# Softplus steps of a selective-scan loop respaced between two engines, D u moved to ScalarE, and a leaner near part

## The chip, the cores and the metric

The kernel runs on one core of a Trainium2 chip. The metric is the device time in microseconds (us) of one execution; the time of a version is the median of its runs. The kernel before takes 2176.8 us, the median of 3 runs from 2174.62 to 2178.04. The profile is of one execution, whose span from the first to the last instruction is 2175.0 us.

Engines are named as in the profile: PE is TensorE, PEld its weight loads, DVE is VectorE, ACT is ScalarE, POOL is GpSimd, and SP is SyncE, which issues the DMAs.

## The reference, cut to what matters

Two layers follow each other on an image x of 64 x 64 pixels with 96 channels. Each normalizes in 32 groups, runs a two-dimensional selective scan (SS2D) and adds the result to x:

```python
x = x + L0(_gn(x))            # softplus, cumulative-sum form, 4 directions, same weights
x = x + L1(_gn(x))            # 4 directions, weights of their own, snake orders

# the core of L1, for direction k, channel d, state n, position t
xz = x @ in_proj_w.T;  xin, z = split(xz)
u  = silu(conv3x3_depthwise(xin) + conv_b)            # 192 channels
dt_r, Bs, Cs = split(x_proj_weight[k] @ u)            # 6 + 16 + 16 rows
delta = softplus(dt_projs_weight[k] @ dt_r + bias[k])
h = h * exp(delta * A) + (delta * u) * B              # A = -exp(A_log), 16 states
y = sum over n of h * C   +   D * u
# then: the four directions are added, layer norm, times silu(z), out_proj
```

In layer 0 the state is written as decay * cumsum(dB_u / (decay + 1e-12)) with decay = exp(cumsum(delta A)), so that positions far along a direction add nothing once the decay has vanished.

## The kernel before, in words

**Layout.** The 192 channels are three tiles T of 128 partitions, each with 64 channels for the upper and the same 64 for the lower half of the image. The 16 states are 8 pairs m.

**Stages.** Each layer has a head (`head`, L885), a scan part and a tail. The head projects, convolves on VectorE (`conv`, L965), applies silu on ScalarE (L981) and starts the output y with D u: `start_y` (L882), called at L986 with GpSimd's multiply, profile line L883. Layer 0 has `near_scans` (L241): only the first NEAR = 192 positions of each direction are scanned, and a flag decides whether `far_scans` (L511) has to run as well; in the profile it does not. Layer 1 has `scans` (L629), the long loop. `scan_weights` (L179) loads the scan weights of a layer: for p in 0, 1 (rows or columns) and d in 0, 1 (forward or backward).

**Near part.** The positions of all four directions are gathered into `nus`, projected (`npj`), and softplus is taken on a tile `npd` of 3 x 384 columns (L339 on). delta, its running sum S and delta u are then written into tiles of twice the size by `both` (L235), four DMAs each, on SyncE: `ndt`, `nS`, `ndu`. VectorE's `nnb` (L441) multiplies by `ndu`.

**Scan loop.** 16 groups k (p, d and a chunk c of the image) x 3 tiles T x 8 pairs m make 384 units; within a group a unit has the slot number 0 to 23. For unit j the stages are:

- `fetch_c`: SyncE loads the row of C, `cb`
- `stage_B`: TensorE spreads the row of B into PSUM (L793, one buffer)
- `stage_a`: ScalarE's exponential m (L802, PSUM, two buffers), VectorE's product b (L806)
- `stage_s`: VectorE's scan h (L815, four buffers), ScalarE's copy of the last column (L820)
- `stage_c`: GpSimd's product hc = h C (L824, five buffers)
- `stage_r`: TensorE adds hc to the output `ys` (L840), five units later

**Prelude.** While a group runs, the operands of the next are prepared: copies of u (`us`, L680), the projection `pj` (L691 copies it to `xd`), the rows B and C, two residuals `rs` (L705, L708), and for each T softplus in five steps: `begin` (TensorE's `pd`, L724, then Abs and Relu on ScalarE, L738 and L739), `logarithm` (ScalarE, four operations, L745 to L748), `lost` (GpSimd, w and ln, L751 and L752), `whole` (GpSimd, sp and su, L755 and L756) and `double` (SyncE, eight DMAs). `pj`, `rs` and `pd` share the two PSUM buffers of m. Each step has a slot; at most one step is taken per slot, in order of the list, and the steps of T = 2 belong to the slots of the next group:

```python
(6, 7, 9, 10, 12, 13, 14, 15, 16, 17, 18, 19, 20, 21, 22),
[copies, project, rows, lambda: residual(0), lambda: residual(1), *delta(0), *delta(1)]
...
return early, list(enumerate(delta(2)))
```

The framework then fixes the order of the instructions in each engine's queue when the program is built; each engine takes its queue in that order.

Of the kernel before, what the change touches and what calls it, by code (L numbers as in the profile page):

```python
# [8 lines left out]
F32 = mybir.dt.float32  # L9
BF16 = mybir.dt.bfloat16  # L10
AF = mybir.ActivationFunctionType
# [32 lines left out]
def two_ss2d_layers(  # L44
# [134 lines left out]
    def scan_weights(l):  # L179

        xw, dwb, am = [], [], []
        for p in range(2):
            lp = 2 * l + p
            w = swp.tile([128, 2, 3, NC], F32, tag=f"xw{p}", name=f"xw{lp}")
            v = swp.tile([128, 2, 3, 128], F32, tag=f"dwb{p}", name=f"dwb{lp}")
            e = swp.tile([128, 2, 3, NS + 1], F32, tag=f"ab{p}", name=f"ab{lp}")
            a = swp.tile([128, 2, 2, 3, NP], F32, tag=f"am{p}", name=f"am{lp}")
            nc.vector.memset(v[96:128], 0.0)  # L190
            for d in range(2):
                r = slice(NB + RK * d, NB + RK * d + RK)
                rr = slice(RK * d, RK * d + RK)
                hi = slice(64 * d, 64 * d + 64)
                c0 = NB + 2 * RK + NS * d
                for half in HALF:
                    for to, of in ((slice(0, NC - NS), slice(0, NC - NS)), (slice(NC - NS, NC), slice(c0, c0 + NS))):
                        nc.sync.dma_start(
                            out=w[half, d, 0:2, to],
                            in_=xpw[lp, :, d, of].rearrange("(b p) c -> p b c", b=2),  # L200
                        )
                        nc.sync.dma_start(out=w[half, d, 2, to], in_=xpw[lp, hi, 2, of])
# [13 lines left out]
                    nc.sync.dma_start(out=e[half, d, 2, :], in_=alb[lp, hi, 2, :])  # L216

            for h, half in enumerate(HALF):
                nc.scalar.activation(a[half, 0], e[half, :, :, h:NS:2], AF.Exp)
            nc.vector.tensor_scalar_mul(a[:, 1], a[:, 0], -0.5)  # L220
            nc.vector.tensor_scalar_mul(a[:, 0], a[:, 0], -1.0)
            xw.append(w)
            dwb.append(v)
            am.append(a)
        return xw, dwb, am
# [6 lines left out]
                out=dst[half], in_=rows[q : q + 1, :].to_broadcast(dst[half].shape)  # L232
            )

    def both(dst, src):  # L235

        for half in HALF:
            for h in range(2):
                nc.sync.dma_start(out=dst[half, ..., h, :], in_=src[HALF[h]])

    def near_scans(weights):  # L241

# [4 lines left out]
        with ExitStack() as sc:  # L247
# [40 lines left out]


            ps = pps.tile([128, 2, 512], F32, tag="m", name="npj")[0:NC, :, 0 : 2 * NEAR]  # L290
            for q in range(2):
                for T in range(3):
                    nc.tensor.matmul(
                        ps[:, q], xw[0:64, 0, T, :], us[0:64, T, q],
                        start=(T == 0), stop=(T == 2),
                    )
# [39 lines left out]
                once.tile([128, 3, 2, 2 * NEAR], F32, name=f"n{nm}") for nm in ("dt", "du", "S")  # L336
            )
            load_exp_ln()
            nc.scalar.activation(w, ps, AF.Abs)  # L339
            nc.vector.tensor_scalar_max(v, ps, 0.0)  # L340
            nc.scalar.activation(w, w, AF.Exp, scale=-1.0)
            nc.scalar.activation(t, w, AF.Identity, bias=one)
            nc.scalar.activation(ln, w, AF.Ln, bias=one)
# [2 lines left out]
            nc.vector.tensor_add(v, v, w)  # L346
            nc.vector.tensor_add(v, v, ln)
            table("exp_and_others")
            both(dt, v)
            nc.vector.tensor_tensor_scan(  # L350
                sums.rearrange("p t w -> p (t w)"), steady.rearrange("p t w -> p (t w)"),
                v.rearrange("p t w -> p (t w)"), 0.0, ALU.mult, ALU.add,
            )
            both(S, sums)
            for h, half in enumerate(HALF):
                nc.gpsimd.tensor_mul(dus[half], v[half], us[half, :, h])
            both(du, dus)

            def four(t, T):
# [99 lines left out]
            def add(j):  # L459
                T, ks = units[j]  # L460
                hc = live.pop(j)[4]
                if ks[0] == 0:
                    live["y"] = pps.tile([128, 2, 512], F32, tag="y", name=f"ny{T}")
                ps = live["y"][:, :, 0 : 2 * NEAR].rearrange("p q (d w) -> p q d w", w=NEAR)
                o = 0
                for i in ks:
                    n, m0, m1 = kinds[i]
                    for m in range(m0, m1):
                        for q in range(2):
                            nc.tensor.matmul(  # L470
                                ps[:, q, :, 0:n], fold2,
                                hc[:, o : o + 2 * n].rearrange("p (d w) -> p d w", w=n),
                                start=(m == 0), stop=(m == NP - 1),
                            )
                            o += 2 * n
                if ks[-1] == len(kinds) - 1:
                    yT = y[T]
                    k = NEAR // HW
                    nears = [
                        (yT[HALF[0], 0:NEAR], ps[HALF[0], 0, 0]),  # L480
                        (yT[HALF[1], L // 2 - NEAR :][:, ::-1], ps[HALF[1], 0, 1]),
                    ]
                    for h, half in enumerate(HALF):
                        nears.append(
                            (columns(yT[half], h, slice(0, k)), of_columns(ps[half, 1, 0], h))
                        )
# [142 lines left out]
    def scans(weights):  # L629

        xw, dwb, am = weights
        with ExitStack() as sc:
# [32 lines left out]
            def prelude(k):  # L665
# [53 lines left out]
                def delta(T):  # L719

                    def begin():
                        ps = spare(f"pd{k}_{T}")[:, 0:HT]
                        for h, half in enumerate(HALF):
# [1 line left out]
                                ps[half], dwb[p][96 : NC + 1, d, T, half],  # L725
                                xd[96 : NC + 1, halves[h]], start=True, stop=True,
                            )
                        me["w"], me["ln"], me["t"] = (
                            pre.tile([128, HT], F32, tag=nm, name=f"{nm}{k}_{T}")
                            for nm in ("w", "ln", "t")  # L730
                        )
                        me["sp"], me["su"] = (
                            pre.tile([128, HT], F32, tag=nm, name=f"{nm}{k}_{T}", bufs=2)
                            for nm in ("sp", "su")
                        )

                        def parts_of_v():
                            nc.scalar.activation(me["w"], ps, AF.Abs)  # L738
                            nc.scalar.activation(me["sp"], ps, AF.Relu)  # L739

                        return parts_of_v


                    def logarithm():
                        nc.scalar.activation(me["w"], me["w"], AF.Exp, scale=-1.0)  # L745
                        nc.scalar.activation(me["ln"], me["w"], AF.Ln, bias=one)
                        nc.scalar.activation(me["t"], me["w"], AF.Identity, bias=one)
                        nc.scalar.activation(me["t"], me["t"], AF.Identity, bias=less1)  # L748

                    def lost():  # L750
                        nc.gpsimd.tensor_sub(me["w"], me["w"], me["t"])  # L751
                        nc.gpsimd.tensor_add(me["ln"], me["ln"], me["w"])  # L752

                    def whole():
                        nc.gpsimd.tensor_add(me["sp"], me["sp"], me["ln"])  # L755
                        nc.gpsimd.tensor_mul(me["su"], me["sp"], me["u"][T])  # L756

                    def double():
                        for nm, of in (("dt", "sp"), ("du", "su")):
                            t = me[nm, T] = pre.tile(  # L760
                                [128, TC], F32, tag=f"{nm}{T}", name=f"{nm}{k}_{T}"
                            )
                            both(t.rearrange("p (h t) -> p h t", h=2), me[of])

                    return [begin, logarithm, lost, whole, double]

                early = list(
                    zip(
                        (6, 7, 9, 10, 12, 13, 14, 15, 16, 17, 18, 19, 20, 21, 22),
                        [  # L770
                            copies, project, rows, lambda: residual(0), lambda: residual(1),
                            *delta(0), *delta(1),
                        ],
                    )
                )
# [109 lines left out]
    def head(l, xT, w):  # L885

        ipw_s, v, ds = w["ipw"], w["v"], w["ds"]
        with ExitStack() as sc:
# [76 lines left out]
            def conv(b, s):  # L965
# [232 lines left out]
```

## Time and profile before

| part of the span, us | length | what VectorE is busy in it | what GpSimd is busy in it |
|---|---|---|---|
| 0 to 103, head of layer 0 | 103 | 85.8 | 37.4 |
| 103 to 198, near part | 95 | 48.1 | 37.2 |
| 198 to 250, tail of layer 0 | 52 | 35.4 | 1.3 |
| 250 to 325, head of layer 1 | 75 | 68.4 | 43.9 |
| 325 to 358, first prelude | 33 | 1.6 | 23.2 |
| 358 to 2124, scan loop | 1766 | 1337.7 | 1121.5 |
| 2124 to 2175, tail of layer 1 | 51 | 28.5 | 2.2 |

Busy time is the time in which an engine executes an instruction. A line of the costliest groups reads: source line, engine, operation, output and inputs, shapes, count; then the total busy time and the mean of one in ns; then the idle time of the engine just before these instructions, and what ended most of it. In the timeline a line has start, duration, engine, source line, operation, and in square brackets the idle time before it with what released it. The mean granted TensorE clock is 0.689 of the full one.

### The profile page before, as it was taken

What the parts mean: (1) busy time and instruction counts of PE and PEld (TensorE: products, weight loads), DVE (VectorE), ACT (ScalarE), POOL (GpSimd) and SP (SyncE); (2) the same over time, 40 slices, a digit from 0 to 9 for tenths busy, and PEclk for the clock granted to TensorE, in tenths of its full rate; (3) what the DMA queues carried; (4) which work ended last, traced back from release to release, by engine and by line L of the source; (5) the groups of instructions that cost most, each with busy time, mean ns of one, the idle gap of its engine ahead of it and who ended that gap; (6) DMA issues with size and microseconds to landing.
All of it is one profiled execution on the core that took longest, in us unless ns stands there. A gap on an engine that the chain in (4) does not pass through costs nothing. (4 is left out here: it accounts for less than half of the span.)

```text
span 2175.0 us, 14719 instructions
## 1 busy us (share of the span) xinstructions
PE 1418.6 (65%) x3694; PEld 369.2 (17%) x3694; DVE 1605.4 (74%) x1108; ACT 881.7 (41%) x1386; POOL 1266.7 (58%) x647
## 2 busy tenths in 40 slices
PE   5337725767676757575757667676767676767678
PEld 3214201111111111111111111111111111111113
DVE  7845793867676868686868777777777777777795
ACT  3343425434343434343443435344434343434333
POOL 0741086575656565656657575757575657574760
PEclk8556866757585858585767776766767676767558
DMA  3243115365555647474838374737473737374663
GB/s 78 77 84 87 39 58 128 106 152 130 146 137 137 155 120 171 116 176 103 188 97 190 101 185 106 185 107 175 113 173 106 180 97 182 103 172 117 154 156 116
DMA packets 130912, 282.88 MB, mean 130 GB/s; under 512 B 45520, under 2 KB 48912, under 8 KB 130720
## 3 DMA queue, kind: packets, MB, share of 16 engines
q1 hardware_dynamic: 128704, 281.06, 53.0%
q10 hardware_dynamic: 2112, 0.79, 0.1%
q8 instruction: 31, 0.51, 0.1%
q14 instruction: 65, 0.53, 0.1%
HBM read 215.75 MB, written 12.13 MB: 105 GB/s over the span
## 5 line engine op out<-in xcount | busy, mean ns | idle before, releaser
L824 POOL TENSOR_TENSOR hc<-h,cb 128x1024 f32<-128x1024 f32 x384 | 895.6, 2353 | 210.2 <-DVE h L815 181.9
L815 DVE TENSOR_TENSOR_SCAN h<-m,carry,b 128x1024 f32<-128x1024 f32 x288 | 673.8, 2343 | 240.4 <-POOL hc L824 219.2
L840 PE MATMUL ys<-hc,fold 128*64 128x512 f32 x1536 | 637.8, 871 | 205.5 <-POOL hc L824 204.7
L806 DVE TENSOR_TENSOR b<-B,du 128x1024 f32<-128x1024 f32 x384 | 469.2, 1222 | 144.8 <-PE B L793 87.7
L802 ACT ACTIVATE m<-dt,am 128x1024 f32<-128x1024 f32 x384 | 428.4, 1116 | 261.7 <-DVE h L815 256.5
L793 PE MATMUL B<-B,selh 96*128 96x512 bf16 x768 | 318.2, 508 | 311.2 <-DVE b L806 310.6
L751 POOL TENSOR_TENSOR w<-w,t 128x512 f32<-128x512 f32 x48 | 60.8, 1267 | 435.3 <-ACT t L748 435.3
L815 DVE TENSOR_TENSOR_SCAN h<-m,b 128x1024 f32<-128x1024 f32 x96 | 218.9, 2284 | 74.2 <-POOL hc L824 66.6
L820 ACT COPY carry<-h 128x1 f32<-128x1 f32 x288 | 54.6, 189 | 503.6 <-DVE h L815 503.1
L840 PEld LDWEIGHTS ys<-hc,fold 128*64 128x64 f32 x1536 | 109.4, 176 | 501.4 <-POOL hc L824 316.0
L793 PEld LDWEIGHTS <-selh 96*128 96x128 bf16 x768 | 70.3, 105 | 730.7 <-issue 727.1
L883 POOL TENSOR_SCALAR y<-u,ds 128x1024 f32<-128x1024 f32 x12 | 98.8, 8246 | 86.7 <-ACT u L981 86.7
L979 DVE SCALAR_TENSOR_TENSOR acc<-pad,v,acc 128x1052 f32<-128x1052 f32 x96 | 121.8, 1334 | 0.3
L835 PE MATMUL ys<-y,ident 128*128 128x256 f32 (+1 forms) x144 | 87.6, 717 | 50.1 <-POOL y L883 37.8
L705 PE MATMUL rs<-xd,ident 96*96 96x512 f32 x128 | 87.7, 775 | 26.7 <-DVE h L815 25.5
L724 PE MATMUL pd<-xd,dwb 29*64 29x512 f32 x192 | 69.9, 815 | 18.2 <-ACT B L715 12.3
L715 ACT CAST B<-rs 32x1024 bf16<-32x1024 f32 x48 | 48.1, 1003 | 70.4 <-PE rs L708 69.7
L752 POOL TENSOR_TENSOR ln<-ln,w 128x512 f32<-128x512 f32 x48 | 60.7, 1264 | 3.7
L755 POOL TENSOR_TENSOR sp<-sp,ln 128x512 f32<-128x512 f32 x48 | 60.7, 1266 | 1.3
L680 ACT COPY us<-u 128x256 f32<-128x256 f32 x48 | 16.7, 403 | 96.5 <-POOL su L756 96.5
L738 ACT ACTIVATE w<-pd 128x512 f32<-128x512 f32 x48 | 28.6, 595 | 65.6 <-PE pd L724 62.7
L845 ACT COPY y<-ys 128x256 f32<-128x256 f32 (+1 forms) x72 | 29.5, 444 | 59.7 <-PE ys L840 59.4
(161 smaller groups left out, 1079.8 us busy)
## 6 DMA issues: line engine op xcount, KB each, us to landing
cb<-C SPq DMA_DIRECT2D x768, 256.0 KB
dt<-sp SPq DMA_DIRECT2D x192, 128.0 KB
du<-su SPq DMA_DIRECT2D x192, 128.0 KB
szd<-sz SPq DMA_DIRECT2D x24, 256.0 KB
szt<-szd SPq DMA_DIRECT2D x24, 256.0 KB
xT<-xs SPq DMA_DIRECT2D x8, 384.0 KB
xs<-xT SPq DMA_DIRECT2D x1, 1536.0 KB
xs<-xT SPq DMA_DIRECT2D x8, 192.0 KB
```

The costliest lines, as they stand in the source:

```text
L705: nc.tensor.matmul(ps[0:NB, s], ident[0:NB, 0:NB], xd[0:NB, s], start=True, stop=False)
L724: nc.tensor.matmul(ps[half], dwb[p][96 : NC + 1, d, T, half], xd[96 : NC + 1, halves[h]], start=True, stop=True,)
L751: nc.gpsimd.tensor_sub(me["w"], me["w"], me["t"])
L793: nc.tensor.matmul(ps[:, s], pick(GROUPS[k][1], m), state[k]["B3"][:, s], start=True, stop=True)
L802: nc.scalar.activation(a, state[k]["dt", T], AF.Exp, scale=am[p][:, 0, d, T, m : m + 1])
L806: nc.vector.tensor_mul(b, live.pop(("B", j)), state[k]["du", T])
L815: nc.vector.tensor_tensor_scan(along(d, h), along(d, a), along(d, b), 0.0 if c == first else carry[:, T, m : m + 1], ALU.mult, ALU.add,)
L824: nc.gpsimd.tensor_mul(hc, live.pop(("h", j)), live.pop(("C", j)))
L835: nc.tensor.matmul(f(live["y"]), ident, view, start=(q == 0), stop=False)
L840: nc.tensor.matmul(ps[half], fold[:, 0:64], v[:, halves[h]], start=False, stop=(m == NP - 1))
L883: mul(y[T][:, s], u[T][:, s], ds[:, T : T + 1])
L979: nc.vector.scalar_tensor_tensor(acc, src, wk, acc, ALU.mult, ALU.add)
```

## The change

It has six parts. (1) In the prelude the slots of softplus steps are set anew: for T = 0, 1 and 2 there are two or three slots between ScalarE's logarithm and GpSimd's first step, and the steps of T = 0 and T = 1 are interleaved; copies, projection, rows and residuals come one slot earlier. As at most one step is taken in a slot and the late steps of T = 2 occupy some, they are taken at slots 8 to 12. The tiles w, ln and t get two buffers, so that two tiles of softplus can be under way; their names carry T for that. The aim is that GpSimd should not stand at a softplus step whose operand ScalarE has not finished. (2) D u in the head runs on ScalarE. (3) `scan_weights` loads for layer 0, where all directions have the same weights, only one of the four parts. (4) `both` takes a queue, and in the near part dt and S are issued by ScalarE. (5) The near part's projection loops over T outside, takes Abs and the maximum per T, and half of delta u is multiplied on VectorE. (6) A condition in the near part is written differently with the same meaning.

```diff
-        for p in range(2):
+        D = 1 + l
+        for p in range(1 + l):
...
-            for d in range(2):
+            for d in range(D):
...
-    def both(dst, src):
+    def both(dst, src, queue=nc.sync):
         for half in HALF:
             for h in range(2):
-                nc.sync.dma_start(out=dst[half, ..., h, :], in_=src[HALF[h]])
+                queue.dma_start(out=dst[half, ..., h, :], in_=src[HALF[h]])
...
-            for q in range(2):
-                for T in range(3):
+            for T in range(3):
+                for q in range(2):
                     nc.tensor.matmul(
...
-            nc.scalar.activation(w, ps, AF.Abs)
-            nc.vector.tensor_scalar_max(v, ps, 0.0)
+            for T in range(3):
+                nc.scalar.activation(w[:, T], ps[:, T], AF.Abs)
+                nc.vector.tensor_scalar_max(v[:, T], ps[:, T], 0.0)
...
-            both(dt, v)
+            both(dt, v, nc.scalar)
...
-            both(S, sums)
+            both(S, sums, nc.scalar)
             for h, half in enumerate(HALF):
-                nc.gpsimd.tensor_mul(dus[half], v[half], us[half, :, h])
+                (nc.gpsimd, nc.vector)[h].tensor_mul(dus[half], v[half], us[half, :, h])
             both(du, dus)
...
-                if ks[-1] == len(kinds) - 1:
+                if ks[0]:
...
-                        me["w"], me["ln"], me["t"] = (
-                            pre.tile([128, HT], F32, tag=nm, name=f"{nm}{k}_{T}")
+                        me["w", T], me["ln", T], me["t", T] = (
+                            pre.tile([128, HT], F32, tag=nm, name=f"{nm}{k}_{T}", bufs=2)
...
-                early = list(
-                    zip(
-                        (6, 7, 9, 10, 12, 13, 14, 15, 16, 17, 18, 19, 20, 21, 22),
-                        [
-                            copies, project, rows, lambda: residual(0), lambda: residual(1),
-                            *delta(0), *delta(1),
-                        ],
-                    )
-                )
-                return early, list(enumerate(delta(2)))
+                early = list(zip((13, 14, 17, 19, 20), delta(0))) + list(
+                    zip((16, 18, 21, 22, 23), delta(1))
+                )
+                early += [
+                    (5, copies), (6, project), (8, rows),
+                    (9, lambda: residual(0)), (11, lambda: residual(1)),
+                ]
+                early.sort(key=lambda at: at[0])
+                return early, list(zip((0, 1, 4, 5, 7), delta(2)))
...
-                start_y(nc.gpsimd.tensor_scalar_mul, ds, b, cut)
+                start_y(nc.scalar.mul, ds, b, cut)
```

More of the change, by code (lines that the diff above doesn't have):

```diff
@@ L189, in scan_weights @@
             a = swp.tile([128, 2, 2, 3, NP], F32, tag=f"am{p}", name=f"am{lp}")
-            nc.vector.memset(v[96:128], 0.0)
-            for d in range(2):
+            nc.vector.memset(v[96:128, 0:D], 0.0)
+            for d in range(D):
                 r = slice(NB + RK * d, NB + RK * d + RK)
@@ L218, in scan_weights @@
             for h, half in enumerate(HALF):
-                nc.scalar.activation(a[half, 0], e[half, :, :, h:NS:2], AF.Exp)
-            nc.vector.tensor_scalar_mul(a[:, 1], a[:, 0], -0.5)
-            nc.vector.tensor_scalar_mul(a[:, 0], a[:, 0], -1.0)
+                nc.scalar.activation(a[half, 0, 0:D], e[half, 0:D, :, h:NS:2], AF.Exp)
+            nc.vector.tensor_scalar_mul(a[:, 1, 0:D], a[:, 0, 0:D], -0.5)
+            nc.vector.tensor_scalar_mul(a[:, 0, 0:D], a[:, 0, 0:D], -1.0)
             xw.append(w)
@@ L727, in begin @@
                             )
-                        me["w"], me["ln"], me["t"] = (
-                            pre.tile([128, HT], F32, tag=nm, name=f"{nm}{k}_{T}")
+                        me["w", T], me["ln", T], me["t", T] = (
+                            pre.tile([128, HT], F32, tag=nm, name=f"{nm}{k}_{T}", bufs=2)
                             for nm in ("w", "ln", "t")
                         )
-                        me["sp"], me["su"] = (
+                        me["sp", T], me["su", T] = (
                             pre.tile([128, HT], F32, tag=nm, name=f"{nm}{k}_{T}", bufs=2)
@@ L737, in parts_of_v @@
                         def parts_of_v():
-                            nc.scalar.activation(me["w"], ps, AF.Abs)
-                            nc.scalar.activation(me["sp"], ps, AF.Relu)
+                            nc.scalar.activation(me["w", T], ps, AF.Abs)
+                            nc.scalar.activation(me["sp", T], ps, AF.Relu)
                         return parts_of_v
                     def logarithm():
[L745 to L748, printed above, removed]
+                        nc.scalar.activation(me["w", T], me["w", T], AF.Exp, scale=-1.0)
+                        nc.scalar.activation(me["ln", T], me["w", T], AF.Ln, bias=one)
+                        nc.scalar.activation(me["t", T], me["w", T], AF.Identity, bias=one)
+                        nc.scalar.activation(me["t", T], me["t", T], AF.Identity, bias=less1)
                     def lost():
-                        nc.gpsimd.tensor_sub(me["w"], me["w"], me["t"])
-                        nc.gpsimd.tensor_add(me["ln"], me["ln"], me["w"])
+                        nc.gpsimd.tensor_sub(me["w", T], me["w", T], me["t", T])
+                        nc.gpsimd.tensor_add(me["ln", T], me["ln", T], me["w", T])
                     def whole():
-                        nc.gpsimd.tensor_add(me["sp"], me["sp"], me["ln"])
-                        nc.gpsimd.tensor_mul(me["su"], me["sp"], me["u"][T])
+                        nc.gpsimd.tensor_add(me["sp", T], me["sp", T], me["ln", T])
+                        nc.gpsimd.tensor_mul(me["su", T], me["sp", T], me["u"][T])
                     def double():
@@ L762, in double @@
                             )
-                            both(t.rearrange("p (h t) -> p h t", h=2), me[of])
+                            both(t.rearrange("p (h t) -> p h t", h=2), me[of, T])
                     return [begin, logarithm, lost, whole, double]
-                early = list(
-                    zip(
-                        (6, 7, 9, 10, 12, 13, 14, 15, 16, 17, 18, 19, 20, 21, 22),
-                        [
-                            copies, project, rows, lambda: residual(0), lambda: residual(1),
-                            *delta(0), *delta(1),
-                        ],
-                    )
-                )
-                return early, list(enumerate(delta(2)))
+                early = list(zip((13, 14, 17, 19, 20), delta(0))) + list(
+                    zip((16, 18, 21, 22, 23), delta(1))
+                )
+                early += [
[4 more added lines that the diff above has]
+                return early, list(zip((0, 1, 4, 5, 7), delta(2)))
             units = [
```

## The prediction, made before the changed kernel was run

> **What bounds the kernel now.** I read the busy shares first, then the 40 slices, the costliest groups with their releasers, and at last the timeline of one stall.
>
> ```profile
> PE 1418.6 (65%) x3694; PEld 369.2 (17%) x3694; DVE 1605.4 (74%) x1108; ACT 881.7 (41%) x1386; POOL 1266.7 (58%) x647
> ...
> L824 POOL TENSOR_TENSOR hc<-h,cb 128x1024 f32<-128x1024 f32 x384 | 895.6, 2353 | 210.2 <-DVE h L815 181.9
> L815 DVE TENSOR_TENSOR_SCAN h<-m,carry,b 128x1024 f32<-128x1024 f32 x288 | 673.8, 2343 | 240.4 <-POOL hc L824 219.2
> ...
> L806 DVE TENSOR_TENSOR b<-B,du 128x1024 f32<-128x1024 f32 x384 | 469.2, 1222 | 144.8 <-PE B L793 87.7
> ...
> L751 POOL TENSOR_TENSOR w<-w,t 128x512 f32<-128x512 f32 x48 | 60.8, 1267 | 435.3 <-ACT t L748 435.3
> ```
>
> No engine is full. The scan loop of layer 1, from 358.1 to 2123.6 us in the timeline, is 81% of the span. VectorE has the longest unavoidable work there: 384 units of b (1.22) and scan (2.34), 3.57 us a unit. The last of the 16 groups, which prepares no successor, takes 85.5 us = 24 x 3.57. The other 15 take 112.0 on average, so 26.5 us of each are waits, and the second and fourth rows name them: scans wait 219.2 us for hc, whose engine itself sits 435.3 us before w for ScalarE's t. This is the timeline of such a stall (the third tile's softplus; start, duration, instruction, idle before it):
>
> ```profile
> 1019.05 1.97 PE L724 MATMUL pd<-xd,dwb 29*64 29x512 f32 x4
> ...
> 1025.02 0.72 ACT L748 ACTIVATE t<-t,less 128x512 f32<-128x512 f32 x1
> 1025.82 1.26 POOL L751 TENSOR_TENSOR w<-w,t 128x512 f32<-128x512 f32 x1 [10.46 <-ACT t L748]
> 1027.15 1.26 POOL L752 TENSOR_TENSOR ln<-ln,w 128x512 f32<-128x512 f32 x1
> 1028.37 2.34 POOL L824 TENSOR_TENSOR hc<-h,cb 128x1024 f32<-128x1024 f32 x1
> 1030.67 1.27 POOL L755 TENSOR_TENSOR sp<-sp,ln 128x512 f32<-128x512 f32 x1
> 1030.75 2.35 DVE L815 TENSOR_TENSOR_SCAN h<-m,carry,b 128x1024 f32<-128x1024 f32 x1 [7.50 <-POOL hc L824]
> ```
>
> GpSimd stands 10.46 us before w with hc queued behind it, and the scan, which has four h buffers, gets its buffer only when that hc is done. Thus a softplus step that stands ahead of an hc in GpSimd's order and waits for ScalarE stops VectorE four scans later. From the starts of the scans, averaged over groups, the gaps above 3.57 us are: after scan 8 5.6, 10 5.0, 12 4.0, 13 4.5 (projection and residual), 15 8.4 (tile 0's softplus), 18 4.2, 19 7.9, 20 4.9 (tile 1), 23 13.4 (tile 2), next group 4 4.3. (22 has 2.3 and 0 has 4.9 in the last group too.)
>
> [...] here the records are of two kinds, a pd of 1.07 or 1.97 us, a ys unit of 1.0 or 1.9, a B pair of 0.6 or 1.0, and the mean granted clock is 0.69. [...]
>
> **The change part by part.** *Softplus spacing.* Work is neither added nor removed: 15 preludes x 12 GpSimd steps of 1.27 and 18 ScalarE steps of 0.6 to 0.7. Only positions change. In the changed program's order (groups 2 to 15), GpSimd holds: tile 0: hc9, w, ln, sp, hc10, su; tile 1: hc13, w, ln, sp, su, hc14; tile 2: hc22, w, ln, hc23, sp, su, hc0 of the next group. Before, these stood between hc11 and hc12; around hc16; and around hc20. ScalarE's last t stands after m15, m18 and m1 (before: m16, m20, m1). So for tiles 0 and 1 GpSimd's steps and ScalarE's both move earlier, and only for tile 2 is the distance really larger. I cut a group at five points (S start, E end of a scan) and follow each chain with durations of before.
>
> 1. E8 to S14. Before: 5.6+3.6+5.0+3.6+4.0+4.5-2.34 = 24.0. After: the projection (pj), both residuals (rs) and pd0 come in five consecutive slots, each taking one of the two PSUM buffers of m. pj at E8; rs0 after E10 (+7.1) with B12 inside it, done at 11 to 12.8 (rs 2.4 warm, 4.6 cold); its two casts of about 0.9: 12.9 to 14.7; rs1 and its cast: 16.5 to 20; pd0, Abs, Relu, Exp: 20 to 24; m15 1.1, ln and both t 2.1: t0 at 23 to 27.8. Then w, ln, sp 3.8, hc10 2.35, and S14 follows: 30 to 34.4. I take 32.0.
> 2. S14 to S18. Before 3.6+8.4+3.6+3.6 = 19.2. After: m17 once scan 16 is done (+9.5), m18 behind it (11.7), ln, t, t (13.9), four GpSimd steps 5.1, hc14 2.35, S18: 21.4 to 22.3, I take 21.8. pd1 is read by then and hides under scans 14 to 16.
> 3. S18 to E22. Before 4.2+7.9+4.9+3.6+2.3 = 22.9. After, no softplus lies in it: 4 x 3.57 + 2.34 = 16.6, with leftovers 17.0.
> 4. E22 to S28. Before 2.3-2.34+13.4+4.9+3 x 3.6 = 29.0. After: TensorE holds five ys units in a row ahead of pd2. Warm they take 5 us and pd2 1.1, all under scans 22 to 24; cold they take up to 9.8 and 2.0 and push m1 by 5 us. Then ln, t, t, w, ln, hc23 (7 us), sp, su, hc0 (4.9), and scan 28 also needs B28, which stands behind ys of hc0 (1.0 to 1.9, B 0.6 to 1.0, b 1.2). 21.8 warm, 28.4 cold; I take 24.5[...].
> 5. S28 to E32. Before 4.3+3 x 3.6+2.3 = 17.4. After 17 to 19 (doubled dt, du later, ys start behind), I take 18.0.
>
> Before: 112.5 (112.0 unrounded). After: 32.0+21.8+17.0+24.5+18.0 = 113.3. The stalls are not removed but moved: tile 2's shrinks, tile 0's grows since its chain now starts directly behind the projection. So +1.3 for 14 groups, +18. The first prelude inside the loop has another order (w0 after hc12, w1 after hc14), in which these waits mostly vanish: -7. The extra w, ln, t buffers remove reuse waits that the trace does not show on the path: nothing.
>
> *D u on ScalarE.* It removes
>
> ```profile
> L883 POOL TENSOR_SCALAR y<-u,ds 128x1024 f32<-128x1024 f32 x12 | 98.8, 8246 | 86.7 <-ACT u L981 86.7
> ```
>
> from the groups, and with it this wait in the timeline of the loop's start:
>
> ```profile
> 323.45 2.08 PE L835 MATMUL ys<-y,ident 128*128 128x512 f32 x2 [37.76 <-POOL y L883]
> ```
>
> 12 x 8.25 us on GpSimd, and adds 12 x about 1.13 us on ScalarE[...], which has idle time in both heads (35.6 busy of 103, 26.0 busy of 75 us). The TensorE wait of 37.8 looks large, but u's last tile itself comes at about 324, six convolutions of VectorE being the limit, and xd is copied at 329.8: 1 us won at the loop's start (between -3 and +1).
>
> *Near part.* One of four weight halves is loaded for layer 0. GpSimd's two halves of du (7.42 us together) become one there (3.7) and one on VectorE; ScalarE issues dt and S, so du on SyncE is no longer behind them:
>
> ```profile
> 129.74 3.61 SPq L239 DMA_DIRECT2D ndt<-nv  x4
> 129.79 7.42 POOL L356 TENSOR_TENSOR ndus<-nv,nus 64x1152 f32<-64x1152 f32 x2 [4.08 <-DVE nv L347]
> 134.84 3.47 SPq L239 DMA_DIRECT2D nS<-nsums  x4
> 138.41 3.58 SPq L239 DMA_DIRECT2D ndu<-ndus  x4
> 149.27 2.15 DVE L441 TENSOR_TENSOR nnb<-nB,ndu 128x768 f32<-128x768 f32 x3 [4.17 <-DMA ndu<-ndus]
> ```
>
> du is issued about 3.6 us earlier, and its landing, 11 us after issue, starts nnb. Against it: the reduction for the flag (1.8) now stands behind nnb, a D u of 1.1 us precedes the last nus copy, and Abs per tile adds two fixed costs. The projection's loop order changes no matmul (8.0 us, TensorE-bound). Net -2 (-5 to 0). Fewer weights: about 1 us of memsets and Exp in the first head, hidden under its convolutions.
>
> Sum: 2176.8 + 18 - 7 - 1 - 2 = 2184.8, taken as 2185.
>
> **The rivals.** *TensorE stays warm in all chains*: S14 at 31, segment 4 at 22, the last at 17: 108.8, or 109 a group. 2176.8 - 3 x 14 - 10 = 2125. For it: in the packed slots TensorE has nearly unbroken work; half of the pd records of before are warm. Against it: during a stall nothing feeds TensorE[...]. *TensorE cold throughout*: 34.4+22.0+17.2+28.0+18.0 = 119.6; 2176.8 + 7.5 x 14 - 10 = 2272. For it: pd in the stall shown is 1.97[...].
>
> **How the numbers follow.** Likeliest, stalls moved: 0.48, centred on 2185, some 20 wide. Warm: 0.40, at 2125. Cold: 0.12, at 2270. The ends of each segment partly average; the range 2115 to 2245 holds warm, likeliest and the milder half of cold. Warm and the likeliest's lower end give faster 0.44; a band of 4 us to each side of 2176.8 lies in the likeliest's width: 0.09; slower 0.47.
>
> **What would show it.** In the changed profile: the gap before scan 14 at about 13 us, named after hc; that before scan 18 at 7; that after scan 23 down from 9.8 to 4 or 5; no gap at 8, 10 and 12; group length 113 (first 105); w's wait for t still some 400 us; L883 gone from GpSimd, the first scan at about 354 to 357. It is wrong if scan 14's wait is under 9, or if pd2 waits behind the ys for over 8 us.

## The result, and the profile after

The changed kernel takes 2157.64 us (median of 4 runs, 2156.55 to 2158.35) against 2176.66 us (4 runs): a ratio of 0.9913, with a 95% interval of 0.9896 to 0.993. It is 19 us faster; the prediction had 2185 us and slower as likeliest. The profiled span fell from 2175.0 to 2156.5 us.

The busy shares and the costliest groups of the kernel after, in the columns known from before:

```profile
PE 1354.3 (63%) x3694; PEld 370.7 (17%) x3694; DVE 1598.7 (74%) x1108; ACT 894.0 (41%) x1395; POOL 1161.7 (54%) x634
...
L826 POOL TENSOR_TENSOR hc<-h,cb 128x1024 f32<-128x1024 f32 x384 | 895.0, 2350 | 173.5 <-DVE h L817 145.4
L817 DVE TENSOR_TENSOR_SCAN h<-m,carry,b 128x1024 f32<-128x1024 f32 x288 | 674.3, 2345 | 215.8 <-POOL hc L826 178.7
...
L808 DVE TENSOR_TENSOR b<-B,du 128x1024 f32<-128x1024 f32 x384 | 466.7, 1215 | 166.6 <-PE B L795 118.0
...
L753 POOL TENSOR_TENSOR w<-w,t 128x512 f32<-128x512 f32 x48 | 60.7, 1265 | 552.5 <-ACT t L750 454.0
```

GpSimd lost the 99 us of y, and VectorE is as busy as before. Scans wait 178.7 us for hc instead of 219.2, b waits more for B, and GpSimd still stands 454.0 us (435.3 before) before w for ScalarE's t. The aim of the new slots, a GpSimd that does not stand, was thus not met. The timeline of tile 0's stall in one group of the kernel after shows the same chain as the one of before:

```profile
843.29 0.72 ACT L750 ACTIVATE t<-t,less 128x512 f32<-128x512 f32 x1
844.09 1.26 POOL L753 TENSOR_TENSOR w<-w,t 128x512 f32<-128x512 f32 x1 [18.28 <-ACT t L750]
845.42 1.26 POOL L754 TENSOR_TENSOR ln<-ln,w 128x512 f32<-128x512 f32 x1
846.76 1.26 POOL L757 TENSOR_TENSOR sp<-sp,ln 128x512 f32<-128x512 f32 x1
847.99 2.34 POOL L826 TENSOR_TENSOR hc<-h,cb 128x1024 f32<-128x1024 f32 x1
850.28 1.26 POOL L758 TENSOR_TENSOR su<-sp,u 128x512 f32<-128x512 f32 x1
850.36 2.29 DVE L817 TENSOR_TENSOR_SCAN h<-m,b 128x1024 f32<-128x1024 f32 x1 [9.20 <-POOL hc L826]
```

GpSimd stands 18.28 us before w, and scan 14 waits 9.20 us for the hc behind sp. From the starts of the scans, the gap before scan 14 is now 14.6 us and that before scan 18 is 10.7, that is 11.0 and 7.1 above the 3.57 of a unit, where the prediction expected 13 and 7; those after scans 8, 10 and 12 are gone. What stood after scan 23 is down from 9.8 to 0.2 above a unit, further than the 4 or 5 expected, but 4.0, 1.0 and 2.1 us now stand after scans 2, 3 and 5 of the next group. The account of the two profiled executions, in us:

| stretch | before | after | difference | predicted |
|---|---|---|---|---|
| up to the first scan | 358.1 | 351.3 | -6.9 | -3 |
| first scan to the end of scan 8 | 37.2 | 37.1 | -0.1 | 0 |
| first cycle, from the end of scan 8 to that of the next group | 108.5 | 99.1 | -9.4 | -7 |
| the 14 cycles after it | 1567.4 | 1564.9 | -2.5 | +18 |
| end of the last group's scan 8 to the last scan | 52.4 | 53.2 | +0.7 | 0 |
| tail | 51.4 | 51.0 | -0.4 | 0 |
| sum | 2175.0 | 2156.5 | -18.5 | +8 |

And one of the 14 cycles, as a mean, by the prediction's five segments:

| segment | before | predicted | after |
|---|---|---|---|
| 1: E8 to S14 | 23.8 | 32.0 (30 to 34.4) | 30.3 |
| 2: S14 to S18 | 19.1 | 21.8 | 22.0 |
| 3: S18 to E22 | 22.9 | 17.0 | 17.4 |
| 4: E22 to S28 | 28.9 | 24.5 (21.8 to 28.4) | 23.3 |
| 5: S28 to E32 | 17.4 | 18.0 | 18.7 |
| sum | 112.0 | 113.3 | 111.8 |

### The profile page after: what moved, and what is told of

Read it like the earlier page. It is cut to its first block, busy times and chain, and to the rows that moved or that the text cites. A ratio compares the mean times of both kernels' runs of the same rounds, so it can differ in the third digit from the quotient of the medians.

```text
span 2156.5 us, 14481 instructions
## 1 busy us (share of the span) xinstructions
PE 1354.3 (63%) x3694; PEld 370.7 (17%) x3694; DVE 1598.7 (74%) x1108; ACT 894.0 (41%) x1395; POOL 1161.7 (54%) x634
## 5 line engine op out<-in xcount | busy, mean ns | idle before, releaser
L817 DVE TENSOR_TENSOR_SCAN h<-m,carry,b 128x1024 f32<-128x1024 f32 x288 | 674.3, 2345 | 215.8 <-POOL hc L826 178.7
L842 PE MATMUL ys<-hc,fold 128*64 128x512 f32 x1536 | 599.8, 834 | 336.9 <-POOL hc L826 336.2
L795 PE MATMUL B<-B,selh 96*128 96x512 bf16 x768 | 310.9, 497 | 271.1 <-DVE b L808 270.6
L753 POOL TENSOR_TENSOR w<-w,t 128x512 f32<-128x512 f32 x48 | 60.7, 1265 | 552.5 <-ACT t L750 454.0
L707 PE MATMUL rs<-xd,ident 96*96 96x512 f32 x128 | 69.3, 624 | 38.5 <-ACT xd L693 26.6
L726 PE MATMUL pd<-xd,dwb 29*64 29x512 f32 x192 | 65.0, 760 | 3.3 <-ACT sp L741 2.2
L717 ACT CAST B<-rs 32x1024 bf16<-32x1024 f32 x48 | 48.1, 1002 | 14.4 <-PE rs L710 13.8
L837 PEld LDWEIGHTS ys<-y,ident 128*128 128x128 f32 x144 | 33.1, 272 | 74.1 <-ACT y L847 46.4
```

What stands on the lines that cost most here:

```text
L707: nc.tensor.matmul(ps[0:NB, s], ident[0:NB, 0:NB], xd[0:NB, s], start=True, stop=False)
L726: nc.tensor.matmul(ps[half], dwb[p][96 : NC + 1, d, T, half], xd[96 : NC + 1, halves[h]], start=True, stop=True,)
L753: nc.gpsimd.tensor_sub(me["w", T], me["w", T], me["t", T])
L795: nc.tensor.matmul(ps[:, s], pick(GROUPS[k][1], m), state[k]["B3"][:, s], start=True, stop=True)
L817: nc.vector.tensor_tensor_scan(along(d, h), along(d, a), along(d, b), 0.0 if c == first else carry[:, T, m : m + 1], ALU.mult, ALU.add,)
L837: nc.tensor.matmul(f(live["y"]), ident, view, start=(q == 0), stop=False)
```

## The experiments

**Do the parts add?** The first two kernels divide the change: the new slots with the two buffers of w, ln and t, put into the kernel before; and everything else. (The expectations call the former part 5; in the list of the change above it is the first.)

> The kernel before with part 5 alone (new slots of the prelude, two buffers for w, ln, t). Theory A (the gain has two sources that add: the loop, whose first group got 9.4 us shorter and the other fourteen together 2.5, and the stages ahead of it, 6.9 us): 2176.7 - 12 = 2165, first scan still at 358, scan groups 2 to 15 at 111.8. Rival B (the loop is shorter because it starts from another state, so that the parts do not add): 2157 or 2176.

> The changed kernel without part 5 (D u on ScalarE, one weight part for layer 0, the near part's edits). Theory A: 2176.7 - 7 = 2170, first scan at 351, groups at 112.0 as before. Rival B: no change at all, 2177.

The spacing alone: 2166.18 us, ratio 0.9959 (0.9945 to 0.9973); first scan at 358.6, first cycle 98.9, the others 111.84. Everything else: 2168.84 us, 0.9974 (0.9966 to 0.9983); first scan at 349.6, cycles 111.99. In the profiled spans the two parts bring -9.8 and -9.2 us, in sum -19.0, and the whole change -18.5. The medians give -8.0 and -5.3, in sum -13.3 against -19.0, a difference within the intervals. First scans and cycles are within 2 us of those of the changed kernel, so the parts are taken to add and are studied one by one. The spacing's gain is the first cycle's, and next to nothing in the 14 others.

**Is it the order on GpSimd?** The next edit adds and removes no work. `keep` adds, for an instruction, an edge to the previous one of the code on the same engine, so that the built order of hc and the softplus steps is the order of the code:

```diff
+            keep = tc.keep_in_program_order
...
-                        nc.gpsimd.tensor_sub(me["w", T], me["w", T], me["t", T])
+                        keep(nc.gpsimd.tensor_sub(me["w", T], me["w", T], me["t", T]))
...
-                nc.gpsimd.tensor_mul(hc, live.pop(("h", j)), live.pop(("C", j)))
+                keep(nc.gpsimd.tensor_mul(hc, live.pop(("h", j)), live.pop(("C", j))))
```

> The changed kernel, with the four softplus operations and hc of the loop held on GpSimd in the order in which the code states them; in the built order w then stands behind hc15, hc19 and hc2 instead of hc9, hc13 and hc22. No work is added or removed. Theory A (the stalls come from softplus steps that stand on GpSimd ahead of an hc and wait for ScalarE): the gaps before scans 14, 18 and 27 vanish, a group takes 88 to 95 us, in all 1830 to 1920 us. Rival B (TensorE's projection, residuals and pd, or ScalarE, set the pace, and GpSimd only shows it): the waits move to m or B, groups stay at 108 or more, 2110 or more.

> The kernel before with the same pin and the old slots: w stands behind hc13, hc18 and hc0. Theory A: the order on GpSimd matters, not the spacing of the slots, so the old slots do nearly as well: groups of 88 to 97 us, 1860 to 1960 us. Rival C (the wider spacing is needed once the order is right, since ScalarE's t comes one unit after its slot): T0 and T1 keep stalls of 4 to 6 us each, groups of 97 to 104, 1960 to 2060. Rival B: 2140 or more.

Pinned, the changed kernel takes 1851.67 us, 0.851 (0.8494 to 0.8525), and the kernel before 1879.62 us, 0.8643 (0.8629 to 0.8658). The mean cycle is 90.4 and 92.2 us. The groups of the changed kernel, pinned:

```profile
L818 DVE TENSOR_TENSOR_SCAN h<-m,carry,b 128x1024 f32<-128x1024 f32 x288 | 674.1, 2344 | 41.3 <-ACT m L805 24.9
...
L754 POOL TENSOR_TENSOR w<-w,t 128x512 f32<-128x512 f32 x48 | 61.0, 1272 | 97.3 <-ACT t L751 97.3
```

and tile 0's softplus in its timeline:

```profile
958.29 0.72 ACT L751 ACTIVATE t<-t,less 128x512 f32<-128x512 f32 x1
958.51 2.36 POOL L827 TENSOR_TENSOR hc<-h,cb 128x1024 f32<-128x1024 f32 x1 [2.92 <-DVE h L818]
...
962.08 2.35 POOL L827 TENSOR_TENSOR hc<-h,cb 128x1024 f32<-128x1024 f32 x1 [1.21 <-DVE h L818]
963.19 2.34 DVE L818 TENSOR_TENSOR_SCAN h<-m,carry,b 128x1024 f32<-128x1024 f32 x1
964.39 1.28 POOL L754 TENSOR_TENSOR w<-w,t 128x512 f32<-128x512 f32 x1
965.74 1.27 POOL L755 TENSOR_TENSOR ln<-ln,w 128x512 f32<-128x512 f32 x1
966.78 2.34 DVE L818 TENSOR_TENSOR_SCAN h<-m,carry,b 128x1024 f32<-128x1024 f32 x1
```

ScalarE's t ends at 959.0, and w starts at 964.39 without a wait, two hc later; no scan waits. Over the whole run these scans wait 41.3 us, most of it for m, and w's 97.3 us are one wait before the loop's first softplus, when GpSimd has nothing else. The pin could have changed the order on other engines too. The traces say that it did not in the six cycles after the first: VectorE, ScalarE and TensorE take the same instructions in the same order in the changed kernel and in its pinned form, GpSimd alone differs, and the mean of these cycles falls from 110.9 to 90.5 us. (Later cycles differ on ScalarE as well, in where copies of u stand, and gain as much.) This shows what one trace alone only suggested: 21 us of each cycle were set by the order of GpSimd's queue, not by an engine's work, and rival B falls. The old slots do nearly as well once pinned, so rival C falls too. The two pinned kernels are 28 us apart in the medians and 24.6 in the profiles; of the latter 5.3 lie ahead of the first scan, where the other parts act, 22 in the loop, and the tail takes 2.9 back. In the loop segment 1 is 21.0 with the new slots instead of 23.9 with the old ones (projection and residuals), and segment 5 is 18.7 instead of 17.4.

**The parts ahead of the loop.** D u on ScalarE alone (part 2 of the change), one weight part alone (part 3), and the near part's edits alone (parts 4, 5 and 6), each in the kernel before.

> The kernel before with D u on ScalarE alone. Of the 6.6 us by which the last silu of the first head came earlier in the changed kernel, theory A gives this edit the part in which VectorE's convolution products ran longer beside GpSimd's y (1.33 to 1.44 us instead of 1.24): 1.9 us in the first head, 0.7 in the second, so 2 to 3 us, 2172, less up to 1.2 for the D u ahead of the last nus copy. Rival B (the whole 7 us are this edit's, since GpSimd's 99 us are gone): 2167 to 2168.

> The kernel before with one of four weight parts for layer 0 alone. Theory A: VectorE no longer waits 2.1 us for ScalarE's Exp and its table load inside the first convolution, and the memset and the rest leave its queue (1.0), a table load leaves the last silu's way (0.8): 3 to 4.5 us, 2170. Rival B (hidden under the convolutions, as the prediction had it): 2174.

> The kernel before with the near part's edits alone (two queues, half of delta u on VectorE, Abs per tile, loop order). Theory A: S, issued beside du on the other queue, lands 13.5 us after its issue instead of 8.8, and the chain then waits for S instead of du, so the edits win nothing: first scan within 1.5 us of 358, 2172 to 2176. Rival B (the prediction's -2, at most -5, from the earlier issue of du): 2169 to 2172.

Measured: 2170.39 us, 0.9979 (0.9971 to 0.9987); 2170.68 us, 0.9981 (0.9974 to 0.9989); and 2184.25 us, 1.0034 (1.0023 to 1.0046). The first scan comes at 353.0, 353.6 and 361.0 instead of 358.1, that is -5.1, -4.5 and +2.9, in sum -6.7, close to the -6.9 of the changed kernel. Each is read from one execution; in the kernels that have all these edits the first scan lies between 349.6 and 351.3 when nothing is pinned. The times do not add so well: by their ratios they are -4.6, -4.1 and +7.4 us, in sum -1.3, against -5.7 for everything but the spacing. The difference is in the last of the three, which loses time in the loop too (below).

D u lay between the two theories. On ScalarE it takes 1.15 us each (12 in 13.8 us in the changed kernel), where the exponential m of the same size takes 1.12. The first head's stretch of convolutions is 1.6 us shorter (67.1 instead of 68.7), near the 1.9 of theory A. It is not that all products beside y ran longer, as the means of 1.33 to 1.44 us in the expectation suggest: in the records two single products take 2.1 us and are 1.3 without y, all others are alike. And between the second head's last u and the first scan 3.8 us more are gone (29.0 instead of 32.8), where ScalarE, before the projection's copy xd, had stood 3.16 us until GpSimd's y was done. Neither theory had that.

For the weights theory A held: the stretch of convolutions is 64.3 instead of 68.7 us. In the timeline of the kernel before, VectorE's part of it (the multiplication of A waits for ScalarE's Exp, which stands behind a table load from 47.01 to 48.29 us):

```profile
48.58 0.19 DVE L220 TENSOR_SCALAR am<-am 128x48 f32<-128x48 f32 x1 [2.13 <-ACT am L219]
...
97.69 0.70 DVE L190 MEMSET dwb<- 32x768 f32 x1 [0.22 <-issue]
```

The head's last silu starts at 101.94 us, 0.84 after VectorE's last product, since a table load of 1.28 us stands ahead of it.

For the near edits both theories were too kind. Abs and the maximum per tile take 3 x 0.49 and 3 x 0.56 us in the changed kernel, where one of each took 1.13 and 1.36 before. The edits' timeline, with the issuing engines' queues (a line of four issues lasts from the start of the first to the end of the last, waits between them included):

```profile
131.33 3.64 ACTq L239 DMA_DIRECT2D ndt<-nv  x4
...
134.01 6.05 SPq L239 DMA_DIRECT2D ndu<-ndus  x4
...
136.43 7.35 ACTq L239 DMA_DIRECT2D nS<-nsums  x4
143.88 1.92 ACT L429 ACTIVATE nna<-ndt,am 128x768 f32<-128x768 f32 x4 [15.47 <-DMA ndu<-ndus]
...
149.77 1.03 ACT L432 ACTIVATE nnwt<-nS,lneps,am 128x768 f32<-128x768 f32 x1 [3.97 <-DMA nS<-nsums]
```

nna needs only dt, which has landed at 140.30, but starts at 143.88, when the last of ScalarE's own DMA issues is over; before it started at 137.74, as dt had landed. The four issues of S themselves take 0.6 to 1.0 us each, 2.9 in sum. In the other 4.4 of the 7.35 us ScalarE's queue stands: its second issue waits on the semaphore on which the first du transfer reports and starts at 139.68, just after that one has landed (139.65), and its fourth does the same for the second du transfer (143.19, after 143.16). SyncE's 6.05 us likewise hold a wait of 3.1 for VectorE's half of delta u. S lands at 149.8 instead of 143.5, and du at 146.7 instead of 149.2, so that the chain waits for S where it waited for du. The DMA engines are 90% busy or more from 133 to 147 us before, and from 129 to 142 in the changed kernel, which has the same two queues: beside the 2.5 us by which du lands earlier stand the 6.3 by which S lands later. Of the profiled 7.5 us over the kernel before, 2.9 are ahead of the first scan; the rest lies in the loop, which the edits do not touch: segment 1 of the last seven cycles has 24.5 instead of 23.6, with the gap after scan 10 at 5.6 in all of them where it was 3.5 to 4.0 in three. Its runs spread from 2174.7 to 2187.4, so this share is not the edits' own by what these runs show. Issuing all from one queue again tests the first cause:

```diff
-            both(dt, v, nc.scalar)
+            both(dt, v)
...
-            both(S, sums, nc.scalar)
+            both(S, sums)
```

> The near part's edits as in the seventh run, but with dt and S issued by SyncE as before, ahead of du. In that run ScalarE's first near exponential stood behind its eight DMA issues and started at 143.9 instead of 137.7. Theory A (the edits lose because ScalarE, which issues in order, cannot compute meanwhile): that exponential at 137 to 139, first scan at 357 to 359.5 instead of 361, 2172 to 2177. Rival B (Abs per tile, the loop order or the shared multiplication lose it): 361, 2180 or more.

nna starts at 138.5, the first scan at 356.5, 4.5 earlier than with two queues, and the time is 2177.28 us, 1.0006 (0.9998 to 1.0014). The scan and the time lie just beside theory A's ranges, by 0.5 and 0.3 us, and rival B falls: it is the second queue that loses. The remaining near edits then bring 1.6 us in the profile and nothing that the times can tell.

**Two numbers of the prediction's chain.** One buffer more for h, and one less for w, ln and t, both in the changed kernel:

```diff
-                h = live["h", j] = mn.tile([128, TC], F32, tag="h", name=f"h{j}", bufs=4)
+                h = live["h", j] = mn.tile([128, TC], F32, tag="h", name=f"h{j}", bufs=5)
```

> The changed kernel with five instead of four buffers for h. In the built order w then stands behind hc9, hc12 and hc22, and a scan waits for the hc five units earlier. Theory A (in order GpSimd, then the h buffer): T0's wait falls from 11.2 to about 9 us, T1's stays at 7 to 8, T2's 4 falls to 1: groups at 106 to 108, 2065 to 2100. Rival B (the waits are not the buffer's): 2155 to 2160. Rival C (each of the three stalls shrinks by a full unit of 3.57): groups at 101, 1995 to 2005.

> The changed kernel with one buffer each for w, ln and t, as before the change. The built order of the loop is nearly unchanged. Theory A (the second buffers are off the path, as the prediction had it): 2155 to 2160. Rival B (T1's Abs then waits for T0's last step on GpSimd, which is late by now): T1's stall grows by 2 us or more, 2185 or more.

With five h buffers the time is 2168.2 us, 0.9967 (0.996 to 0.9974): not 70 us faster than the changed kernel but 11 slower, outside the ranges of all three theories, with B's the nearest. The timeline of this kernel at tile 0's stall, and at tile 2's in the group after:

```profile
850.56 1.26 POOL L753 TENSOR_TENSOR w<-w,t 128x512 f32<-128x512 f32 x1 [20.79 <-ACT t L750]
...
855.80 6.96 POOL L826 TENSOR_TENSOR hc<-h,cb 128x1024 f32<-128x1024 f32 x3
858.17 2.29 DVE L817 TENSOR_TENSOR_SCAN h<-m,b 128x1024 f32<-128x1024 f32 x1 [7.91 <-POOL hc L826]
```

```profile
909.20 1.98 PE L842 MATMUL ys<-hc,fold 128*64 128x512 f32 x4 [5.28 <-POOL hc L826]
...
911.10 1.03 PE L795 MATMUL B<-B,selh 96*128 96x512 bf16 x2
...
912.17 1.23 DVE L808 TENSOR_TENSOR b<-B,du 128x1024 f32<-128x1024 f32 x1 [2.84 <-PE B L795]
```

Tile 0: the scan's wait is put off by one unit, as it must be with one buffer more, but the builder, which now had room, put all four softplus steps ahead of the hc and the last t behind m16 on ScalarE instead of m15, which takes back what the buffer gave: the gap is 13.9 instead of 14.6. Tile 2: here the scan does not wait for an h buffer at all. The late hc delays its ys on TensorE, B stands behind that ys, and b behind B; the mean gap after scan 2 is 7.1 us (7.6 in the changed kernel, whose timeline has the same three waits in this place). So the wait of tile 2 reaches VectorE over TensorE's queue, and no h buffer can help. That the builder answers a buffer with another order is why a count of buffers does not give the time.

With single buffers for w, ln and t (`bufs=2` taken away again from their tile): 2160.39 us, 0.9935 (0.9919 to 0.9952); the 14 cycles have 111.85 as with two (111.78), only the first has 101.8 instead of 99.1. The medians are 2.8 us apart, and the intervals of the two ratios overlap, so costing these buffers at nothing was right as far as the times tell.

**The other order.** With GpSimd pinned a gap of 5.7 us after scan 5 was left, where the built order of VectorE has two b ahead of one scan, and the second waits for its B. So b and scan are kept in the order of the code too:

```diff
-                nc.vector.tensor_mul(b, live.pop(("B", j)), state[k]["du", T])
+                keep(nc.vector.tensor_mul(b, live.pop(("B", j)), state[k]["du", T]))
...
-                nc.vector.tensor_tensor_scan(
+                keep(nc.vector.tensor_tensor_scan(
```

The second kernel has the same, but `both` and `near_scans` as before the change.

> The changed kernel with GpSimd pinned as in the third run, and VectorE's b and scan of the loop held in program order too. In the third run the built order puts two b ahead of a scan at slot 5 and elsewhere, and that scan then waits for the second B. Theory A: the gap after scan 5 (5.7) falls to 3.6, groups at 87.5 to 89.5 instead of 90.4, 1808 to 1840 us. Rival B (the two b ahead are what keeps VectorE busy while a scan waits): 1852 or more.

> D u on ScalarE, one weight part and the new spacing, with GpSimd and VectorE held in program order in the loop as in the eighth run, and without the near part's edits. Theory A (the near edits cost about 3 us by themselves): first scan at 348 to 350.5, 1836 to 1841. Rival B (they cost nothing beside the others): first scan at 353, 1843.

Measured: 1842.75 us, 0.8478 (0.8463 to 0.8493), cycles 89.4, the gap after scan 5 at 3.6; and without the near edits 1843.33 us, 0.8464 (0.8445 to 0.8484). In the first kernel theory A has the gap and the cycles right, and the time is 3 us above its range; rival B falls. Scans now hardly wait, as their groups in this kernel show:

```profile
PE 1298.4 (71%) x3694; PEld 369.8 (20%) x3694; DVE 1598.2 (87%) x1108; ACT 893.3 (49%) x1395; POOL 1165.3 (63%) x634
...
L818 DVE TENSOR_TENSOR_SCAN h<-m,carry,b 128x1024 f32<-128x1024 f32 x288 | 674.3, 2342 | 2.2 <-ACT carry L823 1.9
...
L818 DVE TENSOR_TENSOR_SCAN h<-m,b 128x1024 f32<-128x1024 f32 x96 | 219.0, 2282 | 1.2 <-ACT carry L823 0.9
```

VectorE is busy 87% of the span. For the near edits theory A missed and rival B held: the tail of layer 0 starts 1.9 us earlier without them (199.4 against 201.3), but the first scan comes at 354.0 against 353.4. By the last u 1.4 us of the lead are gone, and the first prelude, which the pins order as well, takes 1.1 longer (33.5 us from the last u against 32.4). Why, was not followed. Both kernels are the best found, and neither is told from the other.

## Why the prediction was wrong

**What bounds the kernel, and how it stalls: right.** The wait of a scan for the hc that stands behind a softplus step was the prediction's reading of one stall; pinning GpSimd removed 21 us from every cycle and 306 us from the changed kernel. The five segments came out within 0.5 us in 2 and 3, and within 0.8 in 5. That tile 0's stall grows while the projection's gaps go, that tile 2's shrinks, and that w goes on waiting over 400 us, were each forecast and seen. Where tile 2's rest would stand was forecast in kind only: the prediction has scan 28 behind B28 and the ys of hc0, the trace has scan 27 behind B27 and the ys of hc23. GpSimd took its queue in order in these runs: in the kernel after it stood 18.28 us before w while a finished h waited for its hc behind w, and with another order in the queue the scans with a carry wait 41.3 us instead of 215.8.

**The term that decided the sign: the 14 cycles, +18 instead of -2.5.** The step "I take 32.0" for segment 1 failed by 1.7 us, and "I take 24.5" for segment 4 by 1.2, each 14 times: 23 and 17 us, of which segments 2, 3 and 5 give back 19 by being 0.2, 0.4 and 0.7 longer. In both the value was set between a warm and a cold TensorE, that is between rs and pd matmuls of about 0.59 and of about 1.06 us. Counted from E8 of the cycle shown above (819.8), rs0 ends at 10.5, its casts at 14.1, rs1 at 16.9, pd0 at 19.5 and t at 24.2; the prediction had 11 to 12.8 for rs0 and 23 to 27.8 for t. The granted clock rises during pj: in the cycle shown it is 0.50 from 820.5 to 824.2 us, 1.00 from 824.3 to 844.7, which covers the packed slots, and 0.50 from 844.8 to 860.0. In each of the 14 cycles it goes from 0.5 to 1.0 between 1.6 and 3.8 us after pj's start and back 23 to 27 us after it. Accordingly pj's matmuls fall from 1.21 to 0.59 us among its twelve, and those of rs against xd then take 0.59 to 0.67 in every cycle. In the 14 cycles of before, pj starts at 1.0 and the clock falls to 0.5 between 7.6 and 14.1 us after its start; in 9 of them the matmuls of the first residual took 1.06 to 1.17. What makes the clock rise and fall is not shown. The groups, two of before and two of after:

```profile
L705 PE MATMUL rs<-xd,ident 96*96 96x512 f32 x128 | 87.7, 775 | 26.7 <-DVE h L815 25.5 <-ACT xd L691 1.3
L724 PE MATMUL pd<-xd,dwb 29*64 29x512 f32 x192 | 69.9, 815 | 18.2 <-ACT B L715 12.3 <-ACT sp L739 5.0 <-DVE h L815 0.8
...
L707 PE MATMUL rs<-xd,ident 96*96 96x512 f32 x128 | 69.3, 624 | 38.5 <-ACT xd L693 26.6 <-DVE h L817 11.8
L726 PE MATMUL pd<-xd,dwb 29*64 29x512 f32 x192 | 65.0, 760 | 3.3 <-ACT sp L741 2.2 <-DVE h L817 0.8
```

That the packed slots may run warm stood in the prediction, for the rival "TensorE stays warm", and was not followed. The pd of 1.97 us that the prediction held against it was an exception: tile 2's pd matmuls took 0.59 to 0.75 us in 12 of the 14 cycles of before (1.06 to 1.11 in the other two), and 0.59 to 0.64 in all 14 of after. Segment 4 was 22.5 us in the first seven cycles and 24.2 in the last seven; why they differ was not followed.

**The first cycle, -9.4 instead of -7:** right in sign and reason, its size a guess. In this cycle the gaps before scans 14 and 18 are 3.6 and 3.5 us, so its stalls are indeed absent.

**Ahead of the loop, -6.9 instead of -3: three sizes wrong.** Fewer weights were costed at nothing, "hidden under its convolutions"; but the convolutions are themselves the bound of the head, and the multiplications of A and the memset stand in their queue: -4.5 alone. D u was given -1 on the ground that u itself comes late; the first prelude's wait behind y and two of VectorE's products beside GpSimd's y made it -5.1. Its price for y, 8.25 us each, was a mean of 2.8 to 42.3 (last section). The near edits were given -2 for an earlier issue of du; it was overlooked that ScalarE, which issues, must also compute, that an issue can wait for a transfer of the other queue, and that S would become the last to land: +2.9.

So the working had the right chains, and a sum of +8 out of terms from -7 to +18, whose stated bounds were wider than the sum. That the measured time lies in the range says little. The rival on the faster side, given 0.40, had the right cause, but at 2125 us lies 33 below the measured time: its cycle of 108.8 has 22 for segment 4 and 17 for segment 5, where the trace has 23.3 and 18.7.

## What to carry to other kernels

Where an engine serves both a steady stream and an occasional side chain, and takes its queue in order as GpSimd did here (18.28 us before w with an hc behind it), read in the built order what stands ahead of what, and ask for every side step whether its operand is ready when it comes up: here holding one engine to the order of the code was worth 306 us, sixteen times the whole change. A work item that seems hidden under a stage is not hidden if it sits in the queue of the engine that bounds that stage: fewer weights brought 4.5 us here. And ScalarE did not compute while its queue held DMA issues (nna started at 143.88 us instead of 137.74, though dt had landed at 140.30): count an engine's issues as its work, with the transfers that they wait for.

## What the runs showed of the hardware that was not expected

An issue held an engine for a transfer that another engine had issued. With two queues the four issues of S on ScalarE take 2.9 us, as on SyncE before (3.0), but stretch over 7.35, because two of them start only when du transfers issued by SyncE have landed. The second queue brought du's first issue forward, to 134.0 us from 138.4, but S, now under way at the same time as du, lands 13.3 us after its first issue instead of 8.7.

A y on GpSimd took up to 42.26 us beside VectorE. In the heads of the kernel before, VectorE runs convolution products back to back, and this y beside them ends only 0.6 us after the last of them (322.77 us):

```profile
281.13 42.26 POOL L883 TENSOR_SCALAR y<-u,ds 128x1024 f32<-128x1024 f32 x1 [36.62 <-ACT u L981]
...
284.94 14.79 DVE L979 SCALAR_TENSOR_TENSOR acc<-pad,v,acc 128x1052 f32<-128x1052 f32 x12
...
329.63 2.84 POOL L883 TENSOR_SCALAR y<-u,ds 128x1024 f32<-128x1024 f32 x1
```

The same instruction takes 2.84 us once the convolutions are over. In the first head one takes 23.62 us, and two get through in 4.4 and 4.5; what decides this is not shown. That the long one is real and no artefact of the record is seen on TensorE, whose ys waits 37.76 us for it. The products do not slow down meanwhile: 12 in a row take 14.79 us, 1.23 each, as without y. Only three products of 2.05 to 2.09 us stand out in the two heads, each ending shortly before a y does. With D u on ScalarE no product takes over 1.32 us.
